# A window-attention kernel whose norms are summed through HBM and rooted on GpSimd, with its value transposes taken in twos

## Chip, cores and metric

One core of a Trainium2 chip runs the whole program. The metric is the device time of one execution in microseconds (us). The kernel before was run three times: 3805.25, 3806.37 and 3806.59 us, median 3806.37 us. One further execution was recorded by the hardware profiler, and every view and row quoted below comes from that one.

## The reference, cut to what matters

Input x is 1 x 48 x 256 x 256. Two layers, each with a residual. The change lies in the first:

```
t   = groupnorm(x)                       # 16 groups of 3 channels
qkv = depthwise3x3(w_qkv @ t)            # 144 channels, 256 x 256
q, k, v = unfold 4x4 patches of qkv      # 8 heads, 96 rows (6 channels x 16 pixels) by 4096 patches
q = q / max(sqrt(sum over the 96 rows of q*q), 1e-12);  k likewise
out = v @ softmax(temperature * q^T k)^T # per head, 4096 x 4096 scores
x = x + w_proj @ fold(out)
```

The second layer normalises x again and applies three sums of small matrices over width, height and channel inside 64 x 64 windows. The change does not touch it. (Zero patches from the padding of 4 enter the softmax as a constant.)

## The kernel before

**Stages.** (1) Statistics of x and the pointwise convolution of heads 0 and 1 into HBM (t1). (2) `depthwise_first`: the depthwise convolution of head 0, in 10 rows; a row is 126 partitions (7 strips of the image x 18 channels: 6 of q, 6 of k, 6 of v) by 4 x 256 pixels. (3) Attention of the eight heads one after the other, from about 303 to 3331 us in the profile. Beside head h it makes head h+1's depthwise rows. (4) Projection, then (5) the second layer.

**Attention.** A head has 32 blocks of 128 queries, taken as 16 pairs g = 0..15. For each pair TensorE does 48 score matmuls (`logits`, L339: two blocks), ScalarE their exponentials with row sums (L541), VectorE the reciprocal of the sums and the scaled values vn (`normalised`, L554 to L560, four small instructions, once per block), TensorE 4 x 64 matmuls (`weigh`, L570, k = 0..3), and VectorE adds each k to an accumulator (L581, oacc). The PSUM tile `big` has three buffers, used in turn by the four `weigh` groups and the eight score groups. So in heads 1 to 7 the next pair's first score group takes the buffer that the add of k = 1 empties, the second that of k = 2, the third that of k = 3.

**Depthwise rows beside it.** Three rows are in work at once, in different steps: n (row g) gets its first tap on ScalarE (`first`, L215); d (row g - 1) its other eight taps on VectorE (`tap`, L234: three after the first `normalised`, five after the second), its square on ScalarE (L245), its sum over 16 pixels on VectorE (`reduce`, L249, k = 0), its sum over the 6 channels on TensorE (`norm`, L253: 126 x 126 block matrix `same` times 126 x 64, after k = 2), the inverse root by a bit trick and three Newton steps on VectorE (`root`, L257 to L274: 12 instructions of 126 x 64), and `scale` (L279) after k = 3; p (row g - 2) its rounded copy on ScalarE (`high`, L288), the remainder on GpSimd (`low`, L292) and three stores from GpSimd (L297): o at the start of the pair, oh and ol after k = 0. In this stage o, oh and the tile that sq and ol share (tag t4) have one buffer each: `low` waits until `reduce` has read sq.

**Order.** The attention loop stands under `manual_schedule`: each engine's instructions, and each queue's transfers, run in the order in which the loop writes them. What comes ahead of the loop is placed by a scheduler. SP's queue loads queries (L313), values, keys of the next head, depthwise inputs (pad, L209), and in head 0 also the strips of x (xs, L177) and stores of their pointwise result (t1, L195): one strip for each of the 64 weigh groups of head 0, each with two buffers in `big` between them (L183, L186).

**Values of the next head.** In pairs g = 11 to 14 two tiles of 512 values each are loaded at the pair's start (L313, vt) and transposed on TensorE (`turn`, L524: four transposes) and copied by ScalarE (L526), one after k = 0 and one after k = 2.

**Head 0's keys** are loaded by SP and ScalarE's queue in turn, and `depthwise_first` has two buffers for each of o, oh, ol and sq, four for pad.

Of the kernel before, what the change touches and what calls it, by code (L numbers as in the profile page):

```python
# [29 lines left out]
CR = 9  # L30
HC = 3 * C // NH
NP1 = CH * HC
PX = W // KS
# [10 lines left out]
def conv_preact_kernel(  # L44
# [15 lines left out]
    nc = tc.nc  # L60
# [11 lines left out]
    CN = CR * PX  # L72
    t1 = [dram.tile([(h1 - h0) * HC, TR, W + 2], F32, name=f"t1_{h0}") for h0, h1 in GROUPS]
    qkv = [dram.tile([3, CH, HC * KK, CN + PX], F32, name=f"qkv{h}") for h in range(NH)]
    os_ = dram.tile([C * KK, NT], F32, name="os_")
    x1s = dram.tile([C, H, W], F32, name="x1s")

# [26 lines left out]
    for z in range(3):  # L104
        for j in range(CH):
            p = j * HC + z * 6
# [61 lines left out]
    class Strip:  # L168
# [24 lines left out]
        def store(self):  # L193
            for s, rows in enumerate(both_halves(t1[1], 2 * self.j, 2, base=1)):
                nc.sync.dma_start(out=rows, in_=self.ot[:, 2 * s : 2 * s + 2, :])  # L195

    class Depthwise:


        def __init__(self, h, r, pool=None):  # L200
            self.h, self.r = h, r
            self.pool, self.bufs = (pool, 2) if pool else (cv, 1)

        def load(self):
            g = [i for i, (h0, h1) in enumerate(GROUPS) if h0 <= self.h < h1][0]
# [45 lines left out]
        def norm(self):  # L251
            self.pn = one.tile([NP1, PX], F32, name="pn", tag="one")
            nc.tensor.matmul(self.pn, lhsT=same, rhs=self.ss, start=True, stop=True)  # L253

        def root(self, on_scalar=False):
            n = self.pool.tile([NP1, PX], F32, name="n", bufs=2)
            nc.vector.tensor_scalar_max(n, self.pn, 1e-24)  # L257
            y = self.pool.tile([NP1, PX], F32, name="y", bufs=2)
            if on_scalar:
                nc.scalar.activation(n, n, AF.Sqrt)  # L260
                nc.vector.reciprocal(y, n)
# [12 lines left out]
            nc.vector.tensor_scalar(y, y, nmul[:, self.h : self.h + 1], nadd, ALU.mult, ALU.add)  # L274
            self.y = y
# [15 lines left out]
            self.ol = self.pool.tile([NP1, KK, PX], F32R, name="ol", tag="t4", bufs=self.bufs)  # L291
            eng.tensor_sub(self.ol, self.o, self.oh.bitcast(F32))  # L292

        def store(self, parts=(0, 1, 2)):
            px = slice(self.r * PX, (self.r + 1) * PX)
            for i in parts:
                nc.gpsimd.dma_start(  # L297
                    out=qkv[self.h][i].rearrange("j (c k) n -> (j c) k n", k=KK)[:, :, px],
                    in_=self.o if i == 2 else (self.ol if i else self.oh).bitcast(F32),
                )  # L300
# [59 lines left out]
    def depthwise_first():  # L360

        with tc.tile_pool(name="dg", bufs=1) as dg, tc.tile_pool(name="dps", bufs=3, space=PSUM) as dps:
            diag = dg.tile([NP1, 9, NP1], F32, name="diag")
            for t in range(9):
                nc.gpsimd.tensor_scalar_mul(diag[:, t, :], ident[:NP1, :NP1], dwt[:, 0, t : t + 1])
            rows = [Depthwise(0, r, dg) for r in range(CR + 1)]
            for d in rows[:2]:
                d.load()
            for i in range(0, CR + 1, 2):
                a, b = rows[i : i + 2]  # L370
                b.taps_on_tensor(diag, dps.tile([NP1, 2, 512], F32, name="dps"))
                a.first()
                for t in range(1, 9):
                    a.tap(t)
                for d in rows[i + 2 : i + 4]:
                    d.load()
                for d in (a, b):
                    d.square()
                    d.reduce()
                    d.norm()  # L380
                    d.root(on_scalar=True)
                    d.scale()
                    d.high()
                    d.low(nc.gpsimd)
                    d.store()


    with tc.tile_pool(name="xn", bufs=1) as xnp, tc.tile_pool(name="cst", bufs=1) as cst, tc.tile_pool(
        name="nps", bufs=2, space=PSUM
# [109 lines left out]
    with tc.tile_pool(name="ahead", bufs=2) as ah, tc.tile_pool(name="ae", bufs=3) as ae, tc.tile_pool(  # L499
# [91 lines left out]

        load_query(0, 0)
        for m in range(NM):
            load_key(0, m, nc.scalar if m % 2 else nc.sync)
        for m in range(2):
            load_value(0, m)
            turn(0, m)
# [9 lines left out]
        with tc.manual_schedule():  # L607
            load_query(0, 1)
            block = scores(0, 0)
            for h in range(NH):  # L610
                more = h + 1 < NH
                rows = {r: Depthwise(h + 1, r) for r in range(CR + 1)} if more else {}
                for g in range(NG):
# [18 lines left out]
                    elif more:  # L632
                        load_query(h + 1, g + 2 - NG)
                    if p:
                        p.store((2,))
                    if d:
                        for t in range(1, 4):
                            d.tap(t)
# [9 lines left out]

                    if g == 0 and rows:
                        rows[0].load()  # L650
                    if p:
                        p.high()
                    if d:
                        d.square()
                    if n:
                        n.first()
                    for k in range(NK):
                        s = (h * NG + g) * NK + k
                        weigh(h, g, blocks, k)
                        if k == 0 and d:  # L660
                            d.reduce()
                        if k == 0 and p:
                            p.low(nc.gpsimd)
                            p.store((0, 1))
                        for w in strips[s]:
                            w.run(big.tile([128, 2, 512], F32, name="big"))
                        for w in strips[s + 2]:
                            w.load()
                        for w in strips[s - 1] if s else []:
                            w.store()  # L670
                        if k == 2 and d:
# [262 lines left out]
```

## Time and profile before

| what | value |
|---|---|
| median of three runs | 3806.37 us (3805.25 to 3806.59) |
| profiled execution: its own time | 3807.91 us |
| its span | 3806.1 us |
| TensorE matmul busy | 3512.4 us, 92% |
| TensorE weight loads | 2911.7 us, 77% |
| VectorE busy | 2199.7 us, 58% |
| ScalarE busy | 1718.5 us, 45% |
| GpSimd busy | 584.2 us, 15% |
| DMA | 441.66 MB, 116 GB/s over the span |

How to read it: PE is TensorE's matmuls, PEld its weight loads, DVE VectorE, ACT ScalarE, POOL GpSimd; SPq, ACTq, POOLq are the queues that issue transfers. In a timeline a row gives start, length (us), engine, line, operation, output<-inputs, shapes and count; in brackets the idle time of the engine before it and what ended it. Merged rows ("x48") run from the first start to the last end. The chain of waits follows the work that ended last back from the end: each piece is what the next one waited for. A table of windows gives, for stretches of the span, each engine's busy time and in brackets its instructions, then the granted TensorE clock, the busy share of the 16 DMA engines and the GB/s they moved.

### The profile page before, as it was taken

What the parts mean: (1) busy time and instruction counts of PE and PEld (TensorE: products, weight loads), DVE (VectorE), ACT (ScalarE), POOL (GpSimd) and SP (SyncE); (2) the same over time, 40 slices, a digit from 0 to 9 for tenths busy, and PEclk for the clock granted to TensorE, in tenths of its full rate; (3) what the DMA queues carried; (4) which work ended last, traced back from release to release, by engine and by line L of the source; (5) the groups of instructions that cost most, each with busy time, mean ns of one, the idle gap of its engine ahead of it and who ended that gap; (6) DMA issues with size and microseconds to landing.
All of it is one profiled execution on the core that took longest, in us unless ns stands there. A gap on an engine that the chain in (4) does not pass through costs nothing.

```text
span 3806.1 us, 99864 instructions
## 1 busy us (share of the span) xinstructions
PE 3512.4 (92%) x44216; PEld 2911.7 (77%) x44216; DVE 2199.7 (58%) x3520; ACT 1718.5 (45%) x2668; POOL 584.2 (15%) x535
## 2 busy tenths in 40 slices
PE   1866999999999999999999999999999999854998
PEld 0224777788888888888888888888888888712776
DVE  4571776159826972896299439934992222265664
ACT  0223656555545554554455445545554444300232
POOL 0050122012201220122022102210220000000011
PEclk9887999999999999999999999999999999966999
DMA  7475676535433542344244424432443100299784
GB/s 137 153 164 148 177 194 185 173 111 127 108 86 94 127 116 74 104 122 109 84 106 120 98 83 114 119 98 76 123 115 92 41 19 19 47 233 187 126 145 90
DMA packets 280235, 441.66 MB, mean 116 GB/s; under 512 B 57354, under 2 KB 205082, under 8 KB 276336
## 3 DMA queue, kind: packets, MB, share of 16 engines
q1 hardware_dynamic: 225150, 260.52, 26.4%
q0 software_dynamic: 48896, 165.90, 19.4%
q10 hardware_dynamic: 5746, 8.73, 1.0%
q8 instruction: 351, 5.75, 0.6%
q14 instruction: 92, 0.75, 0.1%
HBM read 234.76 MB, written 199.95 MB: 114 GB/s over the span
## 4 chain that ended last, share of the span: by engine, by line
PE 74%; issue 11%; DMA 6%; SPq 1%; DVE 0%; POOL 0%; ACT 0%; POOLq 0%; ACTq 0%
PE big L339 32%; PE big L570 31%; PE pb L832 4%; PE pa L810 2%; PE pc L849 2%; PE big L183 2%; DMA pot<-os__70 1%; DMA pxt<-in_x_dram 1%; PE pst L524 1%; PE pt L587 1%; PE pn L253 1%; DMA x1s<-pxt 1%; DMA t<-ot 1%; DMA kt<-qkv 1%; DMA lxq<-x1s 0%
## 5 line engine op out<-in xcount | busy, mean ns | idle before, releaser
L541 ACT ACTIVATE e<-big,nmx 128x1024 f32<-128x1024 f32 x1024 | 1144.4, 1118 | 843.3 <-PE big L339 634.3
L339 PE MATMUL big<-kt,qt 128*128 128x512 f32 x6144 | 1443.1, 394 | 56.8 <-DMA kt<-qkv 54.5
L570 PEld LDWEIGHTS big<-vn,e 128*64 128x64 f32 x32768 | 1364.6, 137 | 87.8 <-ACT e L541 45.1
L570 PE MATMUL big<-vn,e 128*64 128x96 f32 x32768 | 1422.3, 247 | 9.2 <-ACT ot L186 4.0
L339 PEld LDWEIGHTS big<-kt,qt 128*128 128x128 f32 x6144 | 1147.5, 189 | 322.1 <-issue 62.3
L581 DVE TENSOR_TENSOR oacc<-big,oacc 128x768 f32<-128x768 f32 x480 | 458.0, 954 | 707.7 <-PE big L570 707.7
L234 DVE SCALAR_TENSOR_TENSOR acc<-pad,dwt,acc 126x1024 f32<-126x1024 f32 x600 | 779.2, 1300 | 34.0 <-ACT acc L215 18.2
L292 POOL TENSOR_TENSOR ol<-o,oh 126x1024 fp32r<-126x1024 f32 x80 | 190.1, 2376 | 908.3 <-DVE ss L249 808.7
L554 DVE TENSOR_REDUCE zt<-zs 128x1 f32<-128x4 f32 x256 | 38.9, 152 | 367.9 <-ACT e L541 367.9
L541 ACT ACTIVATION_READ_ACCUMULATOR e<-big,nmx 128x1 f32 x1024 | 196.0, 191 | 0.0
L817 DVE TENSOR_TENSOR lzt<-pa,cbias 128x864 f32<-128x864 f32 (+1 forms) x88 | 136.9, 1626 | 99.7 <-PE pa L810 99.7
L297 POOL DMA_DIRECT2D qkv<-o x80 | 101.1, 1264 | 565.7 <-DVE zu L556 339.9
L839 ACT COPY lyt<-pb 128x512 f32<-128x512 f32 x144 | 84.5, 586 | 215.7 <-PE pb L832 215.7
L245 ACT ACTIVATE sq<-acc 126x1024 f32<-126x1024 f32 x75 | 79.3, 1058 | 172.2 <-issue 111.7
L279 DVE TENSOR_TENSOR o<-acc,y 126x1024 f32<-126x1024 f32 x75 | 149.5, 1993 | 10.5 <-DMA qkv<-o 10.5
L832 PEld LDWEIGHTS pb<-wsb,lzt 128*64 128x64 f32 x2304 | 125.8, 138 | 28.4 <-issue 20.3
L715 PE MATMUL pps<-pot,wp 96*96 96x512 f32 x128 | 80.2, 797 | 71.4 <-DMA pot<-os__70 71.4
L832 PE MATMUL pb<-wsb,lzt 128*64 128x128 f32 x2304 | 141.8, 279 | 1.9 <-issue 1.9
L186 ACT ACTIVATE ot<-big,bias 108x1024 f32<-108x1024 f32 x64 | 71.1, 1113 | 145.6 <-PE big L183 76.9
L590 POOL DMA_DIRECT2D os__70<-oo x64 | 32.7, 516 | 616.5 <-ACT oo L589 616.4
L715 PEld LDWEIGHTS pps<-pot,wp 96*96 96x96 f32 x128 | 27.2, 220 | 123.8 <-issue 116.2
L215 ACT ACTIVATE acc<-pad,dwt 126x1024 f32<-126x1024 f32 x75 | 85.3, 1137 | 72.7 <-DMA pad<-t 72.7
(115 smaller groups left out, 1888.7 us busy)
## 6 DMA issues: line engine op xcount, KB each, us to landing
pad<-t SPq DMA_DIRECT2D x80, 761.9 KB
qkv<-o POOLq DMA_DIRECT2D x80, 504.0 KB, 7.0
qkv<-oh POOLq DMA_DIRECT2D x80, 504.0 KB, 7.4
qkv<-ol POOLq DMA_DIRECT2D x80, 504.0 KB, 9.1
t<-ot SPq DMA_DIRECT2D x128, 217.7 KB
qt<-qkv SPq DMA_DIRECT2D x176, 96.0 KB
xs<-in_x_dram SPq DMA_DIRECT2D x128, 96.0 KB
os__70<-oo POOLq DMA_DIRECT2D x64, 192.0 KB, 2.9
```

The source lines that it names most:

```text
L215: nc.scalar.mul(self.acc, self.pad[:, 0:KS, 0:W], dwt[:, self.h, 0:1])
L234: nc.vector.scalar_tensor_tensor(self.acc, self.pad[:, dy : dy + KS, dx : dx + W], dwt[:, self.h, tap : tap + 1], self.acc, ALU.mult, ALU.add,
L279: nc.vector.tensor_tensor(self.o.rearrange("p (a b) x -> p a b x", a=KS), self.acc.rearrange("p a (x b) -> p a b x", b=KS), self.y.rearran ...
L292: eng.tensor_sub(self.ol, self.o, self.oh.bitcast(F32))
L297: nc.gpsimd.dma_start(out=qkv[self.h][i].rearrange("j (c k) n -> (j c) k n", k=KK)[:, :, px], in_=self.o if i == 2 else (self.ol if i else ...
L339: nc.tensor.matmul(ps[:, i, :], lhsT=qt[:, r, q0 : q0 + 128], rhs=kts[2 * j + i][:, r // 2, :], start=(r == 0), stop=(r == 2),)
L541: nc.scalar.activation(e[:, j * 1024 : (j + 1) * 1024], ps.rearrange("p a b -> p (a b)"), AF.Exp, bias=nmx[:, b : b + 1], accum_out=zs[:, ...
L570: nc.tensor.matmul(ps[p : p + 64, j // 4, j % 4 * HD : (j % 4 + 1) * HD], lhsT=e[:, mb * 128 + p : mb * 128 + p + 64], rhs=vn, start=(i == 0),
L581: nc.vector.tensor_add(oaccs[h, k], ps[:, :, : 4 * HD], oaccs[h, k])
L715: nc.tensor.matmul(ps[:, i : i + 2, :], lhsT=wp, rhs=ot[:, ki * KS + i : ki * KS + i + 2, :], start=True, stop=True,)
L817: nc.vector.tensor_tensor(zv[:, :, y0 : y0 + n, :], pa[:, :, : n * T3 * C].rearrange("p s (y k) -> p s y k", y=n), cbias.rearrange("p (u v ...
L832: nc.tensor.matmul(pb[s * WS : (s + 1) * WS, i, :], lhsT=zts[u][:, t * C + c + i, :], rhs=wsb[:, t, :], start=True, stop=True,)
```

## The change

Five edits, all in the first layer:

1. In the attention loop the channel sum leaves TensorE: after `reduce` (now at k = 1) SP stores ss (126 x 64) to an HBM buffer and loads it back so that each partition gets the six rows of its group (`gather`). The row's matmuls with `same` go.
2. In the next pair, VectorE sums the six (one reduction of 126 x 64 from 6), and GpSimd does the whole root: 16 instructions of 126 x 64, each on the result of the one ahead (`root_beside`). `scale` moves to the next pair's k = 0, after the add of k = 0; `high`, `low` and all three stores to its k = 1, after `reduce` of the following row; `first` to k = 1. So a row takes one step later in the pair than before, and acc lives over two pairs.
3. The two `turn`s of a pair both stand at k = 0.
4. `depthwise_first` has four buffers (eight of pad); oh and o are stored from SP, ol from GpSimd. Its norm and root stay on TensorE, ScalarE and VectorE.
5. Head 0's keys are loaded by ScalarE's queue, SP and GpSimd in turn.

```diff
+    ssd = [dram.tile([NP1, PX], F32, name=f"ssd{i}") for i in range(2)]
...
-            self.pool, self.bufs = (pool, 2) if pool else (cv, 1)
+            self.pool, self.bufs = (pool, 4) if pool else (cv, 1)
...
+        def gather(self):
+            to = ssd[self.r % 2]
+            nc.sync.dma_start(out=to, in_=self.ss)
+            self.sg = self.pool.tile([NP1, 6, PX], F32, name="sg")
+            nc.sync.dma_start(
+                out=self.sg,
+                in_=to.rearrange("(g u c) n -> g u (c n)", u=1, c=6).to_broadcast([NP1 // 6, 6, 6 * PX]),
+            )
+
+        def root_beside(self):
+            n = self.pool.tile([NP1, PX], F32, name="n", bufs=1)
+            nc.vector.tensor_reduce(n, self.sg.rearrange("p c n -> p n c"), AX.X, ALU.add)
+            y = self.pool.tile([NP1, PX], F32, name="y", bufs=1)
+            z = self.pool.tile([NP1, PX], F32, name="z", bufs=1)
+            nc.gpsimd.tensor_scalar_max(n, n, 1e-24)
+            nc.gpsimd.tensor_scalar(
+                y.bitcast(mybir.dt.int32), n.bitcast(mybir.dt.int32), -0.5, 1597463007.0, ALU.mult, ALU.add
+            )
+            nc.gpsimd.tensor_scalar_mul(n, n, -0.5)
+            for _ in range(3):
+                nc.gpsimd.tensor_mul(z, y, y)
+                nc.gpsimd.tensor_mul(z, z, n)
+                nc.gpsimd.tensor_scalar_add(z, z, 1.5)
+                nc.gpsimd.tensor_mul(y, z, y)
+            nc.gpsimd.tensor_scalar(y, y, nmul[:, self.h : self.h + 1], nadd, ALU.mult, ALU.add)
+            self.y = y
...
                     d.high()
+                    d.store((0,), nc.sync)
                     d.low(nc.gpsimd)
-                    d.store()
+                    d.store((1,))
+                    d.store((2,), nc.sync)
...
-            load_key(0, m, nc.scalar if m % 2 else nc.sync)
+            load_key(0, m, (nc.scalar, nc.sync, nc.gpsimd)[m % 3])
...
                     if p:
-                        p.store((2,))
+                        p.root_beside()
                     if d:
                         for t in range(1, 4):
                             d.tap(t)
...
-                    if p:
-                        p.high()
                     if d:
                         d.square()
-                    if n:
-                        n.first()
                     for k in range(NK):
                         weigh(h, g, blocks, k)
-                        if k == 0 and d:
+                        if k == 0 and p:
+                            p.scale()
+                        if k == 1 and d:
                             d.reduce()
-                        if k == 0 and p:
+                            d.gather()
+                        if k == 1 and p:
+                            p.high()
                             p.low(nc.gpsimd)
-                            p.store((0, 1))
+                            p.store()
+                        if k == 1 and n:
+                            n.first()
                         ...
-                        if k == 2 and d:
-                            d.norm()
-                            d.root()
                         if k == 2 and g + 1 in rows:
                             rows[g + 1].load()
-                        if k == 3 and d:
-                            d.scale()
...
-                        if more and CR + 2 <= g < CR + 6 and k in (0, 2):
-                            turn(h + 1, (g - CR - 2) * 2 + k // 2)
+                        if more and CR + 2 <= g < CR + 6 and k == 0:
+                            for m in range(2):
+                                turn(h + 1, (g - CR - 2) * 2 + m)
```

More of the change, by code (lines that the diff above doesn't have):

```diff
@@ L253, in norm @@
             nc.tensor.matmul(self.pn, lhsT=same, rhs=self.ss, start=True, stop=True)
+        def gather(self):
[23 more added lines that the diff above has]
+            self.y = y
         def root(self, on_scalar=False):
-            n = self.pool.tile([NP1, PX], F32, name="n", bufs=2)
+            n = self.pool.tile([NP1, PX], F32, name="n", bufs=min(self.bufs, 2))
             nc.vector.tensor_scalar_max(n, self.pn, 1e-24)
-            y = self.pool.tile([NP1, PX], F32, name="y", bufs=2)
+            y = self.pool.tile([NP1, PX], F32, name="y", bufs=min(self.bufs, 2))
             if on_scalar:
@@ L292, in low, with store @@
             eng.tensor_sub(self.ol, self.o, self.oh.bitcast(F32))
-        def store(self, parts=(0, 1, 2)):
+        def store(self, parts=(0, 1, 2), eng=nc.gpsimd):
             px = slice(self.r * PX, (self.r + 1) * PX)
             for i in parts:
-                nc.gpsimd.dma_start(
+                eng.dma_start(
                     out=qkv[self.h][i].rearrange("j (c k) n -> (j c) k n", k=KK)[:, :, px],
```

## The prediction

> **What bounds the kernel now.** I read the page's totals, then the merged chain of waits inside one head, then the busy times of single pairs.
>
> ```profile
> PE 3512.4 (92%) x44216; PEld 2911.7 (77%) x44216; DVE 2199.7 (58%) x3520; ACT 1718.5 (45%) x2668; POOL 584.2 (15%) x535
> ```
>
> ```profile
> 1172.39 11.10 PE big L339 x48
> 1183.49 8.07 PE big L570 x192
> 1191.56 0.36 PE pn L253 x2
> 1191.92 2.79 PE big L570 x64
> 1194.72 11.10 PE big L339 x48
> ```
>
> In the chain TensorE follows on TensorE: a pair with a row takes 1194.72 - 1172.39 = 22.33 us, without a gap. From about 786 to 2850 us only TensorE's own work counts. Yet VectorE is nearly as full in these pairs, which its 58% hides (windows of two pairs: PE, PEld, DVE, ACT, POOL):
>
> ```profile
> 2011.25:2033.58 22.33, 22.33 (x307) 19.86 (x307) 20.78 (x35) 12.69 (x19) 6.02 (x5) 1.00 0.51 124
> 2033.58:2055.90 22.32, 22.32 (x307) 19.85 (x307) 20.75 (x35) 12.68 (x19) 6.03 (x5) 1.00 0.49 122
> ```
>
> VectorE has 1.6 us to spare in 22.33. Any new wait on it of more than that stops TensorE through the three buffers of big.
>
> **What the skill says, and whether this trace agrees.** (1) The Trainium skill, "SBUF — State Buffer", "Who interferes with whom": a VectorE instruction with two SBUF inputs and a GpSimd instruction that reads SBUF exclude each other, and the later one blocks fully. A tap reads pad and acc, so it counts. The trace shows it in the first stage (timelines of GpSimd and VectorE):
>
> ```profile
> 235.51 2.36 POOL L292 TENSOR_TENSOR ol<-o,oh 126x1024 fp32r<-126x1024 f32 x1 [7.16 <-ACT oh L288]
> ...
> 247.78 3.04 POOL L292 TENSOR_TENSOR ol<-o,oh 126x1024 fp32r<-126x1024 f32 x1 [6.23 <-ACT oh L288]
> ```
>
> ```profile
> 247.34 1.28 DVE L234 SCALAR_TENSOR_TENSOR acc<-pad,dwt,acc 126x1024 f32<-126x1024 f32 x1
> 248.54 0.55 DVE L261 RECIPROCAL y<-n 126x64 f32<-126x64 f32 x1
> 249.00 2.90 DVE L234 SCALAR_TENSOR_TENSOR acc<-pad,dwt,acc 126x1024 f32<-126x1024 f32 x1
> ```
>
> The GpSimd subtraction takes 2.36 alone; begun under a tap it took 3.04, until 2.2 after that tap's end; the next tap, 1.28 alone, took 2.90. (2) "GPSIMD Engine Reference", 3.1: an fp32 tensor_tensor of 2048 takes 4497 ns; with 2376 ns for 1024 here that is 0.26 us fixed plus 2.07 ns an element. The same page, 2.1: dependent GpSimd instructions need a semaphore between them. (3) "DMA: Bandwidth & Descriptors": about 2.0 us fixed per transfer ("Anatomy of one DMA"), and a read of what a transfer wrote must wait for its completion ("Two DMAs through the same engine are not ordered"). Key loads here took 2.6 to 3.5 us in the chain at 306 to 329.
>
> **The change, part by part.**
>
> *Sums off TensorE.* A pair without extras (last head, 3057.61 to 3079.43) takes 21.82, one with a row 22.325: 0.505 (0.36 and the break in the weighted sums). 70 rows: -35.4 us.
>
> *Transposes in twos.* A pair with two separate ones takes 23.10 (1055.12 to 1078.22). A store of eight transposes costs 1.01 in the chain and one of four 0.59, so eight value transposes after four at 0.48 cost some 0.80; 11.13 + 2.79 + 0.80 + 8.07 = 22.79. 0.31 x 28 pairs: -9 us.
>
> *First stage.* The scales at 276.62 and 284.27 waited 10.5 and 5.7 for a store; with four buffers they don't. But the last store landed at 303.4, and from 264 on 6.3 MB moved: at the 190 GB/s of the fullest slices 33 us, so -6. Three queues for keys: 191 to 207 GB/s flow already, -2. Together -8 (0 to -18).
>
> *Sum and root beside the pairs of heads 1 to 6 (the deciding part).* Call R the end of a row's `reduce`. Three things follow it.
> - SP: store of ss, completion, load of sg: two transfers of 2.0 (the skill) to 3.0 (key loads), I take 2.5 each: sg is there at R + 5.0.
> - GpSimd: `low` had to wait for `reduce`; 0.1 + 2.3 (start 2029.26 to next 2031.57) + three issues of 1.14 to 1.3: free at R + 6.0. The root stands behind the stores in its order.
> - VectorE: two adds (0.87 each, start to start) and `normalised` (0.76), then at R + 2.5 it stands before the sum of six and must wait for sg. Behind that wait are all taps. The sum: 384 inputs against 1024 in 1.22, estimate 0.5: R + 5.5.
>
> Now taps (1.30 each) and root alternate. A GpSimd instruction that comes during a tap waits for its end; it then holds the next one for an estimated 0.15 (of the 2376 ns, all but 0.3 blocked; 64 elements are 0.13). Taps 1 to 3: R + 5.5 to 9.7; `normalised` to 10.4; taps 4 to 8 to 17.5. One root instruction passes per tap, one in the `normalised`: nine done at R + 17.8. Seven are left. Price of one in a dependent chain: the line above gives 0.39 at 64 elements; the nine tensor_scalars of 126 elements (L365) stand 0.59 apart; with the semaphore step I take 0.50 (from 0.30 to 0.65). 7 x 0.5 = 3.5: y is ready at R + 21.4 with the hand-over. Then VectorE does `scale` 1.9, the add of k = 1 0.87, `reduce` 1.14: the next R at **R + 25.3**. The circle needs 25.3 us where TensorE needs 21.82. Saved on VectorE are the 12 root instructions (2031.35 to 2034.39, 3.0), counted by leaving them out.
>
> Per head: the first such pair (g = 2) is 0.9 late (in the pair ahead the taps end near 14.5, then add, scale, add and reduce give R near 19.7; so y comes at 19.2 of its own pair; the second score group needs the add of k = 2 by 23.2, so y by 18.3), the next eight 3.5 each: 28.7. Six heads: **+172 us**. Bounds: root instructions at 0.30 and transfers of 2.0: circle 22.6, +38; at 0.65 and 3.0: 27.1, +260.
>
> *Values at g = 11.* Row 8's o now leaves behind oh and ol at k = 1 of g = 10, some R + 5, and lands 7.0 later (page, L297); the value load waits for it on SP, and both transposes stand at k = 0. 2 us a head (0 to 4): +12.
>
> *Head 0.* Pairs are 26.8 long there, which covers most of the circle. But SP, standing in the gather until about R + 3, has behind it the strip for k = 3: it lands at R + 7, the strip's 1.04 ends the pair at R + 8, and R comes 19.75 into the next: 27.75 against 26.3. With the 10 us that transfers took at 423 to 469, I take 20 (0 to 60).
>
> `first` and `high` on ScalarE (45% busy) and o, oh and t4 (stores land by R + 14, needed after R + 17) I cost at nothing; if a store took 4 us more, the square would be late, but `reduce` has the wait for y as cover.
>
> Sum, on the profiled span: 3806.1 - 35.4 - 9 - 8 + 172 + 12 + 20 = 3957.7. Its execution took 3807.91, 1.8 around the span and 1.5 over the median; the median stands 0.3 over the span: **3958 us**.
>
> **Rivals.**
> *The cover holds.* If a root instruction passes in 0.2 or isn't held by taps, and the two transfers take 4 in all, the circle is at most 21.8 and nothing stalls: 3806 - 35 - 9 - 8 = 3754, faster. It decides from a circle under 22.3. For it: saved VectorE time of 3.0, and GpSimd idle at 85%. Against: the 0.59 spacing and the blocked pairs shown.
> *Half way.* Circle 22.6: 3806 - 52 + 38 + 10 = 3802, no change within 0.2%.
> *Head 0 breaks too.* If each gather costs its strip a full 10 us transfer, ten pairs lose 5 to 7 us in place of 2: 4010. For it: transfers of 10 to 12 us there. Against: most pairs of that head show no wait for xs.
> *The sums stay.* The built instruction order has no channel-sum matmul left in the loop (70 before), so this can't be.
>
> **Chances.** Forecast 0.62, cover holds 0.15, half way 0.08 (faster 0.02, same 0.03, slower 0.03), head 0 too 0.15. Faster by over 0.2% (about what measuring can tell from no change): 0.17; within: 0.03; slower: 0.80. The range 3800 to 4050 takes in both bounds of the circle and leaves out the first rival and part of the second.
>
> **What would show it.** Right: pairs of heads 1 to 6 at 24 to 27 us for g = 3 to 10 and 21.82 in the last head; TensorE's score matmuls released by the add of k = 1 or 2, VectorE waiting for sg and then for GpSimd's y; GpSimd instructions stretched to a tap's length. Wrong: pairs of 21.8 with rows; root instructions under 0.3 beside taps; sg within 3 us of `reduce`. Turn pairs at 22.8 would confirm the second part, a first score matmul near 302 the third.

## The result, and the profile after

The changed kernel takes **3972.29 us** (median of four runs, 3965.21 to 3982.02); the kernel before took 3806.48 us beside it (3805.25 to 3809.05). The ratio is 1.0436, with a 95% interval of 1.0411 to 1.0462: slower, as forecast, and 14 us from the forecast of 3958. The profiled execution took 3965.21 us, its span is 3963.4.

The difference of the spans is 157.3 us. Cut at the starts of score runs on TensorE's timeline (from here on a pair g is the time from the start of its score matmuls to the start of the next pair's), it comes from these stages:

| stage | before | after | difference | predicted |
|---|---|---|---|---|
| up to the first full score run | 331.8 | 313.3 | -18.5 | -8 |
| head 0 | 453.9 | 519.8 | +65.9 | +14 |
| heads 1 to 6 | 2183.5 | 2293.9 | +110.4 | +146 |
| the rest | 836.9 | 836.4 | -0.5 | 0 |

(Predicted for head 0: +20 less ten sums of 0.505 and four turn pairs of 0.31. For heads 1 to 6: 172 + 12, less 60 x 0.505 and 24 x 0.31.) That the total is so close is luck: head 0 and the values at g = 11 cost 52 and 34 us more than predicted, the circle of waits some 71 us less, and the first stage saved 10 us more.

The page's totals after. Against before TensorE has lost 140 matmuls and yet shows a little more busy time (below), VectorE has lost 770 instructions, and GpSimd's busy time has more than doubled:

```profile
PE 3530.5 (89%) x44076; PEld 2913.0 (73%) x44076; DVE 2143.9 (54%) x2750; ACT 1722.7 (43%) x2668; POOL 1361.5 (34%) x1651
```

The chain of waits inside a head, at the turn from pair g = 9 to g = 10 of head 6 (start, length, engine, tile, line). Before, it was TensorE on TensorE:

```profile
2973.59 1.91 issue
2975.50 0.95 DVE oacc L613
2976.45 1.13 DVE ss L250
2977.58 0.88 DVE oacc L613
2978.45 0.04 issue
2978.49 9.84 PE big L369 x42
2988.33 8.77 PE big L602 x209
2997.10 0.03 issue
2997.13 2.07 DVE o L309
```

TensorE's scores now wait for the add of k = 2, which stands behind `reduce` (ss), the add of k = 1 and `scale` (o) on VectorE. This closes a circle: a row's `reduce` starts the trip through HBM and the root, the next `scale` waits for that root, and the next row's `reduce` stands behind `scale`. Two pairs by windows, the counterpart of the two shown before:

```profile
2067.46:2091.51 24.05, 22.20 (x305) 19.45 (x305) 20.24 (x24) 12.80 (x20) 18.59 (x20) 1.00 0.46 124
2091.51:2115.63 24.12, 22.18 (x305) 19.45 (x305) 20.23 (x24) 12.80 (x20) 18.67 (x20) 1.00 0.45 124
```

The pair is 24.1 us where it was 22.33. No engine is full: TensorE idles 1.9 us, VectorE 3.8. That is what a circle of waits looks like in a table of busy times.

The circle itself, on VectorE's timeline of the second of these pairs:

```profile
2091.35 1.23 DVE L250 TENSOR_REDUCE ss<-sq 126x64 f32<-126x1024 f32 x1
...
2097.88 0.85 DVE L269 TENSOR_REDUCE n<-sg 126x64 f32<-126x384 f32 x1 [1.53 <-DMA sg<-ssd]
2098.65 3.91 DVE L235 SCALAR_TENSOR_TENSOR acc<-pad,dwt,acc 126x1024 f32<-126x1024 f32 x3
...
2103.24 6.62 DVE L235 SCALAR_TENSOR_TENSOR acc<-pad,dwt,acc 126x1024 f32<-126x1024 f32 x5
2109.78 0.95 DVE L613 TENSOR_TENSOR oacc<-big,oacc 128x768 f32<-128x768 f32 x1
2112.68 2.04 DVE L309 TENSOR_TENSOR o<-acc,y 126x1024 f32<-126x1024 f32 x1 [1.94 <-POOL y L282]
```

and on GpSimd's:

```profile
2097.39 1.46 POOL L327 DMA_DIRECT2D qkv<-o  x1
2098.92 1.23 POOL L272 TENSOR_SCALAR n<-n 126x64 f32<-126x64 f32 x1
2100.23 1.11 POOL L273 TENSOR_SCALAR y<-n 126x64 int32<-126x64 int32 x1
2101.43 1.37 POOL L276 TENSOR_SCALAR n<-n 126x64 f32<-126x64 f32 x1
2102.76 0.29 POOL L278 TENSOR_TENSOR z<-y 126x64 f32<-126x64 f32 x1
2103.13 0.38 POOL L279 TENSOR_TENSOR z<-z,n 126x64 f32<-126x64 f32 x1
...
2110.58 0.29 POOL L278 TENSOR_TENSOR z<-y 126x64 f32<-126x64 f32 x1
2110.95 0.32 POOL L279 TENSOR_TENSOR z<-z,n 126x64 f32<-126x64 f32 x1
...
2112.24 0.40 POOL L282 TENSOR_SCALAR y<-y,nmul,nadd 126x64 f32<-126x64 f32 x1
```

Two waits are new. At 2097.88 VectorE stood 1.53 us before the sum of six, for sg. At 2112.68 it stood 1.94 us before `scale`, for y. Between them GpSimd's instructions of 64 elements take 1.1 to 1.4 us each while taps run (the three at 2098.92 to 2102.8 beside taps 1 to 3) and 0.29 to 0.40 when they do not, with 0.41 from start to start. Over the whole run the two waits are 89.0 us (60 times, 1.5 each) and 104.0 us (54 times, 1.9 each).

In head 0 the picture is another. Waits from 400 to 780 us (total, times, longest):

```profile
ACT ot L187 <- DMA t<-ot: 116.6, 13, 15.9
```

```profile
SPq L259 <- DVE ss L250: 38.9, 8, 8.4
SPq L261 <- DMA ssd<-ss: 10.7, 8, 2.3
```

Before, the first of these was 13.9 us (4 times). SP stands 39 us for `reduce` and 11 us for the store of the sums to land; behind it in its order stand the stores of the strips (t). ScalarE needs a strip's ot buffer again only two strips later, but by then that store has not landed, so ScalarE stands, TensorE with it.

Not all of the loss is standing. Over these pairs of head 0 (from the second score run to the start of head 1) TensorE is busy for 441 us with 4882 matmuls where it was busy for 414 us with 4902, and the mean granted clock is 0.93 where it was 0.99. So some 27 us of head 0's loss are matmuls that ran longer. At g = 11 of the other heads it can be seen beside a single wait (head 6):

```profile
3014.63 0.55 PE L556 MATMUL pst<-ident,vt 96*128 96x96 f32 x4
3020.06 0.87 PE L556 MATMUL pst<-ident,vt 96*128 96x96 f32 x4 [4.87 <-DMA vt<-qkv]
3020.86 9.89 PE L602 MATMUL big<-vn,e 128*64 128x96 f32 x192
```

After the 4.87 us of waiting, 192 `weigh` matmuls take 9.89 us; with the wait removed ("values a pair later" below) they take 8.14. The granted clock of that pair is 0.89, and 1.00 in the two pairs above with their waits of 1.5 us.

### The profile page after: what moved, and what is told of

It reads as the page before. It is cut to its first block, busy times and chain, and to the rows that moved or that the text cites. A ratio compares the mean times of both kernels' runs of the same rounds, so it can differ in the third digit from the quotient of the medians.

```text
span 3963.4 us, 100161 instructions
## 1 busy us (share of the span) xinstructions
PE 3530.5 (89%) x44076; PEld 2913.0 (73%) x44076; DVE 2143.9 (54%) x2750; ACT 1722.7 (43%) x2668; POOL 1361.5 (34%) x1651
## 5 line engine op out<-in xcount | busy, mean ns | idle before, releaser
L369 PE MATMUL big<-kt,qt 128*128 128x512 f32 x6144 | 1472.0, 397 | 148.2 <-DVE oacc L613 82.1
L235 DVE SCALAR_TENSOR_TENSOR acc<-pad,dwt,acc 126x1024 f32<-126x1024 f32 x600 | 780.1, 1301 | 33.2 <-ACT acc L216 17.4
L309 DVE TENSOR_TENSOR o<-acc,y 126x1024 f32<-126x1024 f32 x75 | 153.2, 2042 | 110.8 <-POOL y L282 104.0
L343 POOL DMA_DIRECT2D kt<-qkv x44 | 22.9, 528 | 545.2 <-PE big L369 531.5
L318 ACT CAST oh<-o 126x1024 fp32r<-126x1024 f32 x80 | 83.7, 1046 | 226.2 <-DVE o L309 226.2
L280 POOL TENSOR_SCALAR z<-z 126x64 f32<-126x64 f32 x210 | 173.2, 825 | 18.4
L272 POOL TENSOR_SCALAR n<-n 126x64 f32<-126x64 f32 x70 | 76.1, 1087 | 292.0 <-DVE n L269 287.0
## 6 DMA issues: line engine op xcount, KB each, us to landing
qkv<-o POOLq DMA_DIRECT2D x70, 504.0 KB, 12.1
```

Of the source, the lines that this page charges most:

```text
L235: nc.vector.scalar_tensor_tensor(self.acc, self.pad[:, dy : dy + KS, dx : dx + W], dwt[:, self.h, tap : tap + 1], self.acc, ALU.mult, ALU.add,
L280: nc.gpsimd.tensor_scalar_add(z, z, 1.5)
L309: nc.vector.tensor_tensor(self.o.rearrange("p (a b) x -> p a b x", a=KS), self.acc.rearrange("p a (x b) -> p a b x", b=KS), self.y.rearran ...
L318: nc.scalar.copy(self.oh, self.o)
L369: nc.tensor.matmul(ps[:, i, :], lhsT=qt[:, r, q0 : q0 + 128], rhs=kts[2 * j + i][:, r // 2, :], start=(r == 0), stop=(r == 2),)
```

## The experiments

All times are medians. The runs of the kernel before beside them gave 3802 to 3809. "After" is the changed kernel, 3972.29. The lengths are read from each profiled run's TensorE timeline as above: head 0, the mean pair of g = 3 to 10 and of g = 11 over heads 1 to 6, and these six heads together. A mean can mix pairs of two kinds; where it does, the text says so. Where the values come a pair later (four kernels, "three pairs" and "split root" among them) g = 11 holds no transposes.

| kernel | us | head 0 | g 3-10 | g 11 | heads 1-6 |
|---|---|---|---|---|---|
| before | 3806 | 453.9 | 22.33 | 23.08 | 2183 |
| after | 3972 | 519.8 | 23.93 | 30.43 | 2294 |
| before + turns in twos | 3796 | 450.8 | 22.33 | 22.78 | 2179 |
| before + first-stage edits | 3787 | 457.7 | 22.33 | 23.08 | 2182 |
| before + both | 3777 | 453.5 | 22.33 | 22.77 | 2179 |
| after, one Newton step | 3882 | 528.1 | 22.10 | 29.61 | 2201 |
| after, no trip | 3843 | 496.2 | 22.05 | 29.49 | 2198 |
| after, trip issued at k = 3 | 4022 | 564.6 | 24.13 | 30.37 | 2305 |
| after, values a pair later | 3920 | 513.7 | 23.88 | 22.47 | 2253 |
| after, head 0's trip on GpSimd's queue | 3929 | 477.3 | 24.02 | 30.38 | 2299 |
| after, sum after tap 3 | 3920 | 525.4 | 22.89 | 30.07 | 2244 |
| three pairs | 3895 | 505.2 | 23.35 | 21.84 | 2218 |
| split root | 3873 | 466.4 | 23.97 | 22.46 | 2260 |
| split root, sum after tap 3 | 3752 | 440.0 | 22.00 | 21.81 | 2161 |

**Turns in twos alone**, on the kernel before:

```diff
-                        if more and CR + 2 <= g < CR + 6 and k in (0, 2):
-                            turn(h + 1, (g - CR - 2) * 2 + k // 2)
+                        if more and CR + 2 <= g < CR + 6 and k == 0:
+                            for m in range(2):
+                                turn(h + 1, (g - CR - 2) * 2 + m)
```

> The kernel before with one part of the change: both value transposes of a pair at k = 0. Theory: 28 pairs of 22.79 in place of 23.10 us, -9 us, about 3797. Rival: the transposes wait at k = 0 for the value loads at g = 11 even without the late stores, then 3800 to 3806 and no gain.

Measured 3796.45 against 3804.22: -7.8 us, ratio 0.9978 (0.9967 to 0.9989). The turn pairs are 22.78 us, as worked out (22.79), and without the late stores g = 11 shows no stall.

**The first-stage edits alone**, on the kernel before (with the lines of the change that let the store choose its queue):

```diff
-            self.pool, self.bufs = (pool, 2) if pool else (cv, 1)
+            self.pool, self.bufs = (pool, 4) if pool else (cv, 1)
...
+                    d.store((0,), nc.sync)
                     d.low(nc.gpsimd)
-                    d.store()
+                    d.store((1,))
+                    d.store((2,), nc.sync)
...
-            load_key(0, m, nc.scalar if m % 2 else nc.sync)
+            load_key(0, m, (nc.scalar, nc.sync, nc.gpsimd)[m % 3])
```

> The kernel before with the first-stage edits alone (four buffers, oh and o stored from SP, head 0's keys on three queues). The trace of the changed kernel has its first full score run 18.5 us earlier than the trace before. Theory now: all of that is these edits, so about 3788. The prediction's theory: the stage is held by its bytes, -8 us, about 3798.

Measured 3787.07: -17.2 us, ratio 0.9950 (0.9937 to 0.9962). The 18.5 us seen in the trace are these edits; the prediction's -8 is outside the interval (-14 to -24 us). The edits were not tried one by one.

**Both together**, the two diffs above on the kernel before.

> The kernel before with the first-stage edits and both transposes at k = 0, nothing of the sums or the root. The two alone gave -17 and -8 us. Theory: they add, about 3780. Rival: they overlap or undo each other, above 3787.

Measured 3777.18 against 3802.37: -25.2 us, ratio 0.9926 (0.9905 to 0.9948). They add. What else the change holds, the sums and the root with the steps moved for them, makes the changed kernel 195 us longer than this one.

**One Newton step in place of three**, on the changed kernel:

```diff
-            for _ in range(3):
+            for _ in range(1):
                 nc.gpsimd.tensor_mul(z, y, y)
```

> The changed kernel with one Newton step in place of three, so 8 of the 16 GpSimd instructions a row are left; this leaves out most of the root's exactness. Theory: GpSimd then has its last instruction before VectorE has its last tap, no wait for y is left, the circle falls from 24.0 to VectorE's own 22.7 to 23.0 us, heads 1 to 6 lose 55 to 65 us: about 3910. Rival, that only the trip through HBM stretches the circle: no change, 3965 to 3975. Rival, that GpSimd's root is the whole of it: pairs of 21.8, 110 us less, about 3860.

Measured 3881.77: 90.5 us less, between the theory (about 3910) and the rival that the root is the whole of it (about 3860). The trace has no wait for y left. The mean pair of 22.10 is a mix: 30 of the 48 pairs take TensorE's 21.8. The circle is better read on VectorE, from one `reduce` to the next: 22.25 (median) where the changed kernel takes 24.09. That is 0.4 over TensorE's own pair, and since each head's first rows are early, more than half of the pairs show nothing of it. So VectorE's own steps with the wait for sg take 22.25, and the wait for y (1.9) is the rest. The theory's floor of 22.7 had been set too high; that the trip alone stretches the circle is refuted.

**No trip**, on the changed kernel: sg comes from a constant buffer (sfix, written ahead of the loop with ones), loaded ahead of the store of ss.

```diff
-            nc.sync.dma_start(out=to, in_=self.ss)
             self.sg = self.pool.tile([NP1, 6, PX], F32, name="sg")
             nc.sync.dma_start(
                 out=self.sg,
-                in_=to.rearrange("(g u c) n -> g u (c n)", u=1, c=6).to_broadcast([NP1 // 6, 6, 6 * PX]),
+                in_=sfix.rearrange("(g u c) n -> g u (c n)", u=1, c=6).to_broadcast([NP1 // 6, 6, 6 * PX]),
             )
+            nc.sync.dma_start(out=to, in_=self.ss)
```

> The changed kernel with sg loaded from a constant buffer, at the same place, so that the load waits for no sum; ss is still stored. The channel sum is left out of the norms. Theory: sg is there when VectorE comes to it, the root starts 2.5 to 3 us earlier and the circle falls below TensorE's 21.82: heads 1 to 6 lose 90 to 110 us; SP no longer stands for the store's completion (14 us in head 0) but still for reduce (49 us), so head 0 keeps most of its 66: about 3865 to 3880. Rival, that GpSimd's 16 instructions set the circle whatever sg does: circle 23.5 to 24, about 3955 to 3970.

Measured 3842.86: 129.4 us less by the medians; by the traces 96 in heads 1 to 6 and 24 in head 0. From one `reduce` to the next are 22.29 us (23 of the 48 pairs again take TensorE's 21.8: `reduce` ends 18.7 us into the pair in a head's first row, and pairs stall only once that has grown to some 23), so the circle did not fall below TensorE's pair, as the theory had it. The wait for y is still there, as long as before:

```profile
DVE o L310 <- POOL y L283: 119.8, 58, 2.3
```

It does little harm now, since all of the circle starts earlier. So neither wait alone is "the" cause: taking away either brings the circle from 24.1 to 22.3. The wait for sg is some 1.5 us and that for y 1.9, and the changed kernel has both in a row.

**The sum after tap 3**, on the changed kernel: the same wait for sg, removed without leaving work out.

```diff
-                    if p:
-                        p.root_beside()
                     if d:
                         for t in range(1, 4):
                             d.tap(t)
+                    if p:
+                        p.root_beside()
```

> The changed kernel with one edit: VectorE takes the sum of six after taps 1 to 3 in place of before them. Theory: the wait for sg (1.5 us a pair) leaves VectorE's chain; the root begins 1.6 us later by the clock but has five taps ahead of its end in place of eight, so y comes some 1 to 2 us earlier after reduce: pairs of 22.5 to 23.2 in place of 24.0, heads 1 to 6 lose 40 to 70 us; head 0 loses its sg waits and little else: about 3900 to 3930. Rival, that y follows sg at a fixed distance whatever taps do: the root is later by 1.6 us and the pairs are 25 to 25.6: 4020 or more.

Measured 3919.6: 52.7 us less, with pairs of 22.89 (expected 22.5 to 23.2). In heads 1 to 6 VectorE hardly waits for sg any more (11 us in all) but longer for y, 3.11 us:

```profile
2081.13 0.84 DVE L269 TENSOR_REDUCE n<-sg 126x64 f32<-126x384 f32 x1
2093.27 2.09 DVE L309 TENSOR_TENSOR o<-acc,y 126x1024 f32<-126x1024 f32 x1 [3.11 <-POOL y L282]
```

From the sum to `scale` are 12.1 us where the changed kernel took 14.8: with five taps ahead and not eight, more of the sixteen instructions run at 0.41. Head 0 gains nothing from it (525.4).

**Values one pair later**, on the changed kernel (both edits alike, for `load_value` and for `turn`):

```diff
-                    if more and CR + 2 <= g < CR + 6:
+                    if more and CR + 3 <= g < CR + 7:
                         for m in range(2):
-                            load_value(h + 1, (g - CR - 2) * 2 + m)
+                            load_value(h + 1, (g - CR - 3) * 2 + m)
```

> The changed kernel with the next head's values loaded and transposed one pair later (g = 12 to 15). Theory: the pair g = 11 of 30 to 31 us comes from the value load waiting for the last of three stores; one pair later it has landed, each of 7 heads loses some 7 us: about 3920. Rival: the stall moves with the load, no change, or to g = 12: 3965 to 3975.

Measured 3919.88: 52.4 us less, g = 11 falls from 30.43 to 22.47. The stall doesn't move with the load, but for head 6, where g = 12 grows from 25.7 to 30.0 us; that pair is the longest of its kind before the change too, and what it waits for wasn't tried. The chain of the changed kernel shows what the stall was (head 6, g = 11):

```profile
3005.98 11.18 DMA qkv<-o
...
3017.18 0.30 SPq L343
...
3017.54 2.38 DMA vt<-qkv
...
3020.06 0.89 PE pst L556 x4
```

The store of o, the last of three, takes 11.2 us; SP holds the value load until it has landed, and TensorE's transposes at k = 0 stand behind that.

**The trip issued at k = 3**, on the changed kernel:

```diff
                         if k == 1 and d:
                             d.reduce()
-                            d.gather()
...
+                        if k == 3 and d:
+                            d.gather()
```

> The changed kernel with the store and load of the sums issued after k = 3 in place of k = 1, so that SP does not stand before them while strips wait behind it. Theory: head 0 is 66 us longer than before because SP waits there for reduce (49 us) with strip stores, strip loads and value loads behind it; moved past the strips, head 0 recovers 30 to 55 us, and heads 1 to 6 stay within 20 us of the changed kernel: about 3915 to 3945. Rival: head 0 is longer because sg and y come late for VectorE or because transfers share the bandwidth; then head 0 keeps its 520 us or gets longer, since sg comes later still: 3970 or more.

Measured 4022.39: 50 us more. The theory as stated fell: head 0 is 565 us. The trace gives the reason (SP's timeline, one pair of head 0):

```profile
524.25 0.83 SPq L210 DMA_DIRECT2D pad<-t  x1
525.18 0.86 SPq L178 DMA_DIRECT2D xs<-in_x_dram  x2
526.14 3.48 SPq L196 DMA_DIRECT2D t<-ot  x2
529.72 2.80 SPq L259 DMA_DIRECT2D ssd<-ss  x1
541.92 0.80 SPq L261 DMA_DIRECT2D sg<-ssd  x1
```

Issued behind the 762 KB of pad and two strip stores, the 32 KB of sums land only 9.4 us after their issue ended (541.92 less 532.52), against 1.1 to 2.7 us (mostly 1.1) in the changed kernel, where they are issued at k = 1. sg is late then, VectorE stands before the sum, and behind it are the `vn` that TensorE needs:

```profile
DVE n L269 <- DMA sg<-ssd: 143.2, 9, 17.3
...
PE big L602 <- DVE vn L592: 96.0, 9, 12.5
```

The edit removed one wait and made a larger one, so it could not tell whether SP's standing was the cause. The next one could.

**Head 0's trip on GpSimd's queue**, on the changed kernel: the store ahead of `low`, the load between `low` and the three stores. Other heads keep SP.

```diff
+            eng = nc.gpsimd if self.h == 1 else nc.sync
             to = ssd[self.r % 2]
-            nc.sync.dma_start(out=to, in_=self.ss)
+            eng.dma_start(out=to, in_=self.ss)
```

> The changed kernel where, in head 0 alone, GpSimd's queue and not SP's stores the sums (ahead of low) and loads them back (behind low, ahead of the three stores). Moving both behind k = 3 on SP had made head 0 longer, 565 us, with SP standing 92 us for the store's completion behind the input load; so two causes are left. Theory: what costs head 0 its 66 us is SP standing in order between strips; with SP free, head 0 is 455 to 475 us, heads 1 to 6 unchanged at 2294: about 3910 to 3925. Rival: it is the small transfers' own landing among the strips' transfers, late sg whatever queue issues it, or GpSimd now later with the root; head 0 stays at 510 us or above: 3965 or more.

Measured 3929.17: 43.1 us less, of which 42.5 in head 0 (477.3; expected 455 to 475), heads 1 to 6 as they were (2299). ScalarE's wait for the strip stores falls from 116.6 to 17.5 us:

```profile
ACT ot L187 <- DMA t<-ot: 17.5, 5, 6.6
```

So at least 42 of the 66 us come from the trip on SP's queue, with SP standing in order. And 42 is what is left after a new loss: on GpSimd's queue sg comes later, and VectorE waits 45.3 us for it in head 0, where it waited 2.3 us in the changed kernel. What that costs the last run below shows.

**Three pairs**, on the kernel before with both good edits: the trip at k = 3, the sum after tap 3 of the next pair, `scale` at its k = 2, the copies and stores one pair later still (q is row g - 3; values a pair later as above).

```diff
-                    if p:
-                        p.store((2,))
+                    if q:
+                        q.store((2,))
                     if d:
                         for t in range(1, 4):
                             d.tap(t)
+                    if p:
+                        p.root_beside()
...
-                        if k == 2 and d:
-                            d.norm()
-                            d.root()
+                        if k == 2 and p:
+                            p.scale()
-                        if k == 3 and d:
-                            d.scale()
+                        if k == 3 and d:
+                            d.gather()
```

> The kernel before with the first-stage edits, both transposes at k = 0, and the sums by way of HBM with the root on GpSimd, but spread over three pairs: sums issued at k = 3, summed on VectorE after taps 1 to 3 of the next pair, scale at k = 2 there, rounded copies and stores one pair later still, values loaded and transposed one pair later. Theory: the circle then has no member that VectorE waits for, pairs of heads 1 to 6 take TensorE's 21.82 (22.8 with transposes), head 0 is near before: 3806 - 35 - 9 - 18 = 3744, up to 3770 if head 0 loses some. Rival, that GpSimd's instructions or the extra transfers cost VectorE or TensorE time wherever they stand: pairs of 22.5 to 23.5 and 3800 or more.

Measured 3895.07: refuted, 2.6% over before (ratio 1.0225 to 1.0297). Here too the trip stands behind the pad load, now in all heads:

```profile
1662.54 0.80 SPq L210 DMA_DIRECT2D pad<-t  x1
1664.90 0.32 SPq L259 DMA_DIRECT2D ssd<-ss  x1
1671.42 0.80 SPq L261 DMA_DIRECT2D sg<-ssd  x1
```

6.5 us from the store's issue to the load's, where the changed kernel mostly took 1.4. And `scale` waits for the copies of the row ahead to leave the single o buffer (66.7 us, 37 times, from 1000 to 2900 us). The mean of 23.35 mixes pairs of 21.8 with single ones of up to 28.4. How the loss divides between the two wasn't tried.

**Split root**, on the changed kernel with head 0's trip on GpSimd's queue and values a pair later: GpSimd does the seed and one Newton step, VectorE two steps and the last product (`finish`) ahead of `scale`.

```diff
-            for _ in range(3):
-                nc.gpsimd.tensor_mul(z, y, y)
+            nc.gpsimd.tensor_mul(z, y, y)
...
+            for _ in range(2):
+                nc.vector.tensor_mul(z, y, y)
+                nc.vector.tensor_mul(z, z, n)
+                nc.vector.scalar_tensor_tensor(y, z, 1.5, y, ALU.add, ALU.mult)
```

> The changed kernel with three edits: head 0's sums by GpSimd's queue as in the run beside it, values one pair later, and the root split: seed and one Newton step on GpSimd (7 instructions), two steps and the last product on VectorE (7 instructions, 1.8 us) right ahead of scale. Theory: with half the GpSimd instructions the circle was 21.8 to 22.3, so pairs of heads 1 to 6 are 21.8 to 22.3 and g = 11 is 22.8: heads 1 to 6 2150 to 2175, head 0 455 to 475, 3760 to 3785, at or below the two good edits alone (3777). Rival: VectorE, given 1.8 us back ahead of the last two adds, becomes the bound at 23 or more: 3830 or more.

Measured 3873.24: the rival. The pairs are 23.97. y is never waited for, but the wait of 1.9 has become 1.9 of VectorE's work in the same place, and the wait for sg is still ahead of it:

```profile
1720.73 0.85 DVE L271 TENSOR_REDUCE n<-sg 126x64 f32<-126x384 f32 x1 [1.68 <-DMA sg<-ssd]
```

**Split root, sum after tap 3:** this and one edit more, `p.root_beside()` behind taps 1 to 3, by the diff shown for the sum.

> The run with the split root (head 0's sums by GpSimd's queue, values one pair later, 7 root instructions on GpSimd and 7 on VectorE) and one edit more: VectorE takes the sum of six after taps 1 to 3. There the circle was 24.05 us by VectorE's own steps, of which 1.5 us were the wait for sg. Theory: without that wait VectorE's steps alone are 22.5 us, which is then the pair: heads 1 to 6 about 2175, head 0 455 to 466, about 3780 to 3790, level with the two good edits alone (3777). Rival, that the later sum makes the root late in its turn: pairs of 23.5 to 24 as before that edit, 3860 or more. Rival, that VectorE's small instructions shorten once they no longer stand beside GpSimd's: pairs of 21.82 and 3750.

Measured **3752.35** against 3803.61: ratio 0.9857 (0.9841 to 0.9874), the fastest kernel of the study and faster than before. Most pairs are 21.8 (mean 22.00), which is TensorE's own work. The time is that of the last rival, but its reason isn't what the trace shows: zu and vn beside GpSimd's `low` and its first store's issue are as long as ever, but a tap begins 0.2 us after vn began:

```profile
1988.51 0.73 DVE L597 SCALAR_TENSOR_TENSOR zu<-e,zt 128x1 f32<-128x1 f32 x1
1989.27 0.16 DVE L599 RECIPROCAL rz<-zu 128x1 f32<-128x1 f32 x1
1989.47 0.98 DVE L601 TENSOR_SCALAR vn<-vT,rz 128x96 f32<-128x96 f32 x1
1989.66 3.92 DVE L235 SCALAR_TENSOR_TENSOR acc<-pad,dwt,acc 126x1024 f32<-126x1024 f32 x3
```

The theory had counted that 0.8 us in VectorE's 22.5: less it, 21.7, and from one `reduce` to the next are 21.75 us (median). Head 0 falls to 440.0 from 466.4 by the later sum, and VectorE's wait for sg there from 46.8 to 20.7 us: the edit is the only difference, so with the trip on GpSimd's queue the late sg cost head 0 some 26 us. In the changed kernel the same edit gave head 0 nothing, so these 26 us are no part of its 66; they hid a part of what freeing SP gave. As an estimate, 42.5 + 26.4 = 69 us: the trip on SP's queue accounts for the whole 66. The two edits weren't tried without the split root and the later values.

## Why the prediction was right, step by step

**Sums off TensorE, turns in twos: right.** Pairs with a row and no stall are 21.81 to 21.82 us (g = 1 and 2), the turn pairs 22.78.

**The circle: right in mechanism, too long by 1.2 us.** For the pair shown above, R, the end of `reduce`, is 2092.58, the next R is 2116.70.

| step | predicted | measured |
|---|---|---|
| VectorE stands before the sum | R + 2.5 | R + 3.8 |
| sg there | R + 5.0 | R + 5.3 |
| the sum | 0.5 | 0.8 |
| last tap ends | R + 17.5 | R + 17.3 |
| each tap held by a root instruction | 0.15 | 0 |
| root instructions done up to 0.3 later | 9 | 10 |
| those left, and each | 7 at 0.50 | 6 at 0.41 |
| y | R + 21.4 | R + 20.1 |
| next R | R + 25.3 | R + 24.1 |

The term that was mis-sized is the last stretch of GpSimd's chain, 3.5 us in the sum and 2.5 in the trace: 0.41 us from start to start, where 0.50 was chosen between bounds of 0.30 and 0.65, and six instructions left and not seven, since two pass in the `normalised` (2102.76 and 2103.13 above). The 0.15 per tap was wrong too: the taps' mean is 1301 ns against 1300 before. It hid two errors the other way, the sum (0.8) and sg (5.3).

The prediction cited the Trainium skill, "SBUF — State Buffer", "Who interferes with whom": the later one blocks. The page states the full block of VectorE's two-port modes; of an instruction with two SBUF inputs it says that it contends. In this trace it holds for GpSimd's instructions, which end with the tap, but no tap is made longer by an instruction of 64 elements. The 2.0 us per transfer is the figure of the Trainium skill, "DMA: Bandwidth & Descriptors", "Anatomy of one DMA", for transfers issued from GpSimd, and SP issues these. Here the store took 1.4 us from its issue to the load's, and the load 3.8 from its issue to the sum, so that 2 x 2.5 came out nearly right by the sum of two errors. And two bounds were added up wrongly: by the prediction's own terms the circle's bounds are 22.9 and 27.4, not 22.6 and 27.1. Nothing hung on it.

Over heads 1 to 6 the pairs g = 3 to 10 lost 48 x (23.93 - 21.82) = 101 us in place of 172. VectorE waiting for sg and then for y was the forecast sign, and both are there.

**Values at g = 11: mechanism right, size wrong.** 30.43 against a turn pair of 22.79 is 7.6 us a head in place of 2, 46 us in place of 12 in heads 1 to 6. The step that failed took 7.0 us for o to land, from the page before; as the last of three stores in a row it now takes 12.1 in the page and 11.18 in the chain. In head 6 some 5 of the 7.8 us are the wait for the values, 2 the slower matmuls after it, for which the prediction had no term, and the rest the circle's wait.

**Head 0: the step that failed most.** SP "has behind it the strip for k = 3: it lands at R + 7" gave +20. This counted SP's standing from R on, but of the 50 us shown above 39 lie ahead of R, in the wait for `reduce`. And what stands behind SP is more: strip stores, whose buffers ScalarE needs, and value loads. The loss is 66 us, nearer the rival "head 0 breaks too" (50 to 70), and by stores rather than by loads of strips. Taking the trip from SP's queue was shown to give back 42 us of it, and by the estimate above it is all of it. How much of that TensorE loses standing and how much by its lower clock (27 us more busy time) the prediction didn't ask.

**First stage: mechanism right, size wrong.** The waits of `scale` for buffers, 10.5 and 5.7 us, were read rightly, but capped at 6 us by the argument that the bytes would then bind, at 190 GB/s. From 264 to 304 us before, only 152 GB/s flowed, and the bytes didn't bind, since with more buffers some of them moved earlier (150 to 225 us: 168 and 202 GB/s in two stretches, where 125 and 188 flowed before). The sum of the two, 16.2, came out whole: the last `scale` starts at 267.39 in place of 284.27.

```profile
284.27 1.22 DVE L279 TENSOR_TENSOR o<-dps,y 126x1024 f32<-126x1024 f32 x1 [5.68 <-DMA qkv<-o]
```

```profile
267.39 1.22 DVE L309 TENSOR_TENSOR o<-dps,y 126x1024 f32<-126x1024 f32 x1
```

**The rivals.** "The cover holds" asked for a circle under 22.3; the last experiment has one (21.75), and is faster, but only with the sum moved, the root divided, the values later and head 0's trip on another queue. "Half way" (22.6) wasn't reached by the changed kernel.

## What to carry to other kernels

A step moved to an idle engine is paid in the latency of its chain and not in busy time: close the circle (which result comes back, to whom, one turn later) and compare its length with the bound engine's pair before moving anything. Place the consumer of a round trip behind other work on its engine, and issue the trip's small store ahead of large transfers, on a queue with nothing urgent behind it. Read a circle from one of its steps to the same step one turn later: a mean over pairs hides it where the first pairs still have something in hand. When two waits stand in a row on one circle, taking away either helps by most of its size, and turning a wait into work of the same length on the same engine helps nothing.

## What the runs showed of the hardware

- GpSimd instructions of 126 x 64 take 0.29 to 0.40 us, 0.41 from start to start in a dependent chain; beside VectorE's taps (1.30) about one passes per tap, at 1.1 to 1.4.
- The other way round, in the changed kernel VectorE's small instructions grow beside GpSimd: zu from 0.16 to 0.73, ending with GpSimd's `low` (126 x 1024, 2.4 us), and vn from 0.27 to 0.98, ending with the issue of the store behind it; before, vn stayed at 0.27 beside the issue of o. A tap that follows still starts 0.2 us after vn started. The taps' mean doesn't move (1301 and 1300 ns).
- A load that reads back a store of 32 KB through HBM was issued 1.4 us after the store in most rows (up to 3.0), and where VectorE waits for sg the sum of six starts mostly 4.7 to 7.5 us after `reduce` (median 5.3). Behind a load of 762 KB issued 2.4 us earlier the first step took 6.5 us, and 9.4 us from the end of the store's issue with strip loads and stores in between.
- Matmuls behind a wait of 4.9 us ran longer (192 in 9.89 us in place of 8.14), at a granted clock of 0.89 over the pair; pairs with waits of 1.5 us kept 1.00. No run varied the length of the wait by itself.
